# Where a router's logits are computed: from the transposed sum, or in parts beside q, k and the attention output

## The chip, the cores and the metric

The kernel runs on one core of one Trainium2 chip. Its time is the device time of one execution in microseconds (us). The profile shows one execution of 1613.6 us. Engines are named as in the profile: PE (matrix products), PEld (its weight loads), DVE (vector), ACT (scalar, activations), POOL, and SP, which issues most transfers.

## The reference

One layer over 4096 tokens of 256 features: a dense graph step, then attention, then a mixture of 8 experts of which each token takes two.

```python
x = x + concat([ln(x), adj @ (ln(x) @ neigh_W.T) / deg], -1) @ lin_W.T   # deg = adj row sums + 1
x0 = layernorm(x)                       # no weights
h = rmsnorm(x0, ln1_w)
q, k, v = h @ wq.T, h @ wk.T, h @ wv.T  # 4 heads, 2 of k and v, 64 wide; q and k are rotated
y = causal_softmax(q @ k.T / 8) @ v     # per head
x2 = x0 + y @ wo.T
flat = rmsnorm(x2, ln2_w)               # x2 / sqrt(mean(x2 * x2) + 1e-6) * ln2_w
probs = softmax(flat @ router_w.T)      # 4096 x 8
# the two best of each token, scaled to a sum of 1, weigh the experts
out = sum_e weight_e * ((silu(flat @ w1[e].T) * (flat @ w3[e].T)) @ w2[e].T)
return x + x2 + out
```

What the change uses is that the router is linear in x2 up to one factor per token, the one of the second rmsnorm. So its logits are that factor times (x0 @ R + y @ (wo.T @ R)), where R is router_w.T with its rows scaled by ln2_w.

## The kernel before

All data are float32. The tokens are eight blocks of 512 (`NB`), each four tiles (`TB`) of 128 rows (`P`). The order of the instructions on every engine is the order in which the program issues them; nothing reorders them afterwards. Loops take dictionaries or lists of small functions (`steps`, `later`, `rest`) and call them at set points between the big products, so an operation's place in the stream is written out by hand.

**Graph stage** (`aggregate`, L428). For each block of rows, eight blocks `jb` of the adjacency are multiplied with features, with seven products in place of eight per pair of blocks (`PRODUCTS`). After the seventh pair of products of every `jb` the functions of `steps[jb]` are called. In the first row block these make the features of the next block (`features`, L390; `turned_x`), and `load_rest` at `jb` 3 issues the loads of the attention's weights on SP. In row blocks 1 to 7 they are `qkv` of the block before: statistics at `jb` 0, the normalised input `h0` at 1 (DVE), its transposes at 2 (`transposed`, L321, with two scaled copies by ACT for each half, L329), then per tile `rotate` (one product with 512 columns for q, k and v, L184; v copied out by ACT, L188; the rotation on DVE and POOL) and `turn_heads` (`heads`: three transposes, L212, two copies by ACT, L213 and L214). At the end of a row block ACT copies the first product (L448), and DVE adds up the others and divides by the degrees; a bank of PSUM becomes free for the next row block when its part has been read.

**Attention** (L564 scores, L569 exponentials on ACT, L587 sums on DVE, L599 values). It goes through the blocks in the order 3, 0, 4, 1, 5, 2, 6, 7; the scores of one group of four tiles are issued before the values of the group before. There are two places for other steps in each group, `place_for_steps(2n)` and `(2n+1)`. `last_qkv` brings in block 7's q, k and v in the first of them. `after(b)` lists what follows a finished block: its input normalised again (`inputs`), the output product added (`project`, L634, L638), then `turn` (L653, L657, L666), `logits` (L681), `weigh` (L696), `choose`, `place` and `scatter`, the last four of which pick each token's experts and write its row into lists in memory. Steps that begin with `None` may share a place; the others each take one. All steps that use TensorE outside of scores and values share one bank of PSUM (`p_ms`).

Before, `turn` transposes x2, four 128x128 transposes for half a block, copies them out scaled by ln2 (ACT, into `qT[b]`, which the finished block's q no longer needs), and squares x2 on ACT for the rmsnorm; `logits` then multiplies `qT[b]` with `router_sb`:

```python
                    nc.tensor.matmul(
                        ps[32 * t : 32 * (t + 1), :], router_sb[:, c, :],
                        qT[b][:, c, t * P : (t + 1) * P],
```

The eight results of a token stand in partitions, so `weigh` transposes them back (L694) and multiplies with the factor of the rmsnorm, which POOL makes of the squares (`power`).

**Experts** (L1185 hidden, L1156 and L1237 output, L1094 transposes of a group's rows). Groups of 256 or 128 rows run one after another. While the first nine of them run, the steps of block 7's `after` are called one at a time by `step()`, two inside `hidden`, one behind it and one behind `combine`, and then two calls of `make_table` (DVE) that list the remaining groups. SP issues the loads of rows, `w13` and `w2` in program order. In the first six groups the transposes of the next group's rows share the bank `p_y` with the output product of the group before.

Of the kernel before, what the change touches and what calls it, by code (L numbers as in the profile page):

```python
# [17 lines left out]
P = 128  # L18
N = 4096
C = 256  # L20
# [46 lines left out]
def fast_kernel(  # L67
# [55 lines left out]
    wo_sb = const.tile([P, 2, C], F32, name="wo_sb")  # L123
    wqkv_sb = const.tile([P, 2, 512], F32, name="wqkv_sb")

    router_sb = const.tile([P, 2, 32], F32, name="router_sb")
    nc.gpsimd.memset(router_sb, 0.0)
# [19 lines left out]
    rstd = [const.tile([P, TB, 1], F32, name=f"rstd{b}") for b in range(NB)]  # L147
    both = [const.tile([P, TB, 1], F32, name=f"both{b}") for b in range(NB)]

    x_blocks = x.rearrange("(b t p) c -> b p t c", t=TB, p=P)  # L150
# [29 lines left out]

    def rotated(pool, b, t, hT, pj, ro, r2, cs, sn):

        for c in range(2):
            nc.tensor.matmul(  # L184
                pj, hT[:, c, t * P : (t + 1) * P], wqkv_sb[:, c, :],
                start=(c == 0), stop=(c == 1),
            )
        nc.scalar.copy(vv[b][:, t, :], pj[:, 384:512])  # L188
        qk = pj[:, 0:384].rearrange("p (h s d) -> p h s d", s=2, d=HD // 2)
        nc.vector.tensor_mul(  # L190
            ro.rearrange("p h s d -> p (h s) d"), qk.rearrange("p h s d -> p (h s) d"),
            cs.to_broadcast([P, 12, HD // 2]),
        )
        for s in range(2):
            nc.vector.tensor_mul(  # L195
                r2[:, :, s, :], qk[:, :, 1 - s, :], sn.to_broadcast([P, 6, HD // 2])
            )
        nc.gpsimd.tensor_sub(ro[:, :, 0, :], ro[:, :, 0, :], r2[:, :, 0, :])  # L198
        nc.gpsimd.tensor_add(ro[:, :, 1, :], ro[:, :, 1, :], r2[:, :, 1, :])
        sq = r2.rearrange("p h s d -> p h (s d)")  # L200
        rh = ro.rearrange("p h s d -> p h (s d)")
        nc.gpsimd.tensor_mul(sq, rh, rh)
        nm = pool.tile([P, 6, 1], F32, tag="nm", name=f"nm_{b}_{t}")
        nc.vector.tensor_reduce(nm, sq, AX.X, ALU.add)
        nc.vector.tensor_max(norms, norms, nm.rearrange("p h o -> p (h o)"))

    def heads(b, t, ro, tr):

        rof = ro.rearrange("p h s d -> p (h s d)")
        trf = tr.rearrange("p a b i -> p (a b) i")  # L210
        for m in range(3):
            nc.tensor.transpose(trf[:, m, :], rof[:, m * P : (m + 1) * P], ident)  # L212
        nc.scalar.copy(qT[b][:, :, t * P : (t + 1) * P], trf[:, 0:2, :])  # L213
        nc.scalar.copy(kT[b][:, t * P : (t + 1) * P], trf[:, 2, :])  # L214


    with (
# [50 lines left out]
        def load_rest():  # L268

            nc.sync.dma_start(wqkv_sb, wqkv.rearrange("(c p) o -> p c o", p=P))  # L270
            nc.sync.dma_start(ln1_sb, ln1)
            nc.sync.dma_start(ln2_sb, ln2)

            wo_h = wo_t.rearrange("(j p d) o -> j d p o", j=2, p=2)
            for j in range(2):
                nc.sync.dma_start(wo_sb[j * HD : (j + 1) * HD], wo_h[j])
            nc.sync.dma_start(
                router_sb[:, :, 0:NE], router_t.rearrange("(c p) e -> p c e", p=P)
            )
# [34 lines left out]

        def transposed(src, dst, scale):

            for h in range(2):
                tr = p_tr.tile([P, 2, 2, P], F32, tag="tr", name="tr")
                for t in range(2):
                    for c in range(2):  # L320
                        nc.tensor.transpose(  # L321
                            tr[:, c, t, :], src[:, 2 * h + t, c * P : (c + 1) * P], ident
                        )
                cols = slice(h * 2 * P, (h + 1) * 2 * P)
                if scale is None:
                    nc.scalar.copy(dst[:, :, cols], tr.rearrange("p c t i -> p c (t i)"))
                else:
                    for c in range(2):
                        nc.scalar.activation(  # L329
                            dst[:, c, cols], tr[:, c].rearrange("p t i -> p (t i)"),  # L330
                            AF.Copy, scale=scale[:, c : c + 1],
                        )

# [14 lines left out]
        def turned_x(b):  # L348
            turned[b] = qT[b % 4]
            transposed(inputs.pop(b), turned[b], None)  # L350

# [114 lines left out]
        def qkv(b):  # L466
# [9 lines left out]
            def norm():  # L476
                made["h0"] = gx.tile([P, TB, C], F32, tag="f", name=f"h0_{b}", bufs=1)
                for t in range(TB):
                    normed(made["h0"][:, t, :], b, t, both[b][:, t])

            def turn():

                made["hT"] = qT[b]
                transposed(made["h0"], made["hT"], ln1_sb)

            def rotate(t):
# [6 lines left out]
                    gx, b, t, made["hT"], pj, ro, r2,  # L493
                    tables[b, "cos"][:, t, None, :], tables[b, "sin"][:, t, None, :],
                )
                made[t] = ro

            def turn_heads(t):
                tr = p_tr.tile([P, 2, 2, P], F32, tag="tr", name=f"trq_{b}_{t}")
                heads(b, t, made.pop(t), tr)  # L500

# [26 lines left out]
        for jb in range(NB):  # L528
            for f, b in ((features, jb + 1), (turned_x, jb + 2), (halve, jb + 1), (scales_x, jb + 3)):
                if b < NB or f is halve:  # L530
                    steps[jb].append(lambda f=f, b=b: f(b))
        steps[3].append(load_rest)
        aggregate(0, steps)
        for b in range(1, NB):
# [5 lines left out]
    with (  # L540
# [105 lines left out]

        def turn(b, h):

            x2 = flats[b][:, :, 0:C]
            tr = p_ms.tile([P, 2, 2, P], F32, tag="ms", name=f"trf_{b}_{h}")  # L650
            for t in range(2):
                for c in range(2):
                    nc.tensor.transpose(  # L653
                        tr[:, c, t, :], x2[:, 2 * h + t, c * P : (c + 1) * P], ident
                    )
            for c in range(2):
                nc.scalar.activation(  # L657
                    qT[b][:, c, h * 2 * P : (h + 1) * 2 * P],
                    tr[:, c].rearrange("p t i -> p (t i)"),
                    AF.Copy, scale=ln2_sb[:, c : c + 1],  # L660
                )
            if h == 0:
                squares[b] = ax.tile([P, TB, 1], F32, tag="ss", name=f"ss_{b}")
            for t in range(2 * h, 2 * h + 2):
                sq = ax.tile([P, C], F32, tag="sq", name=f"sq_{b}_{t}", bufs=1)
                nc.scalar.activation(sq, x2[:, t, :], AF.Square, accum_out=squares[b][:, t])  # L666
            if h == 1:
# [8 lines left out]
        def logits(b):  # L676

            ps = p_ms.tile([P, P], F32, tag="ms", name=f"lgT_{b}")
            for c in range(2):
                for t in range(TB):  # L680
                    nc.tensor.matmul(  # L681
                        ps[32 * t : 32 * (t + 1), :], router_sb[:, c, :],
                        qT[b][:, c, t * P : (t + 1) * P],
                        start=(c == 0), stop=(c == 1), skip_group_check=True,
# [3 lines left out]
            nc.scalar.copy(lgT, ps)  # L688
            picks[b] = squares.pop(b), lgT

        def weigh(b):
            ri, lgT = picks[b]
            lg = p_ms.tile([P, TB, 32], F32, tag="ms", name=f"lg_{b}")
            nc.tensor.transpose(lg.rearrange("p t e -> p (t e)"), lgT, ident)  # L694
            pr = small("r_p", b)
            nc.vector.tensor_mul(pr, lg[:, :, 0:NE], over(ri))  # L696
            top = small("r_top", b, 1)
# [42 lines left out]
        def place(b):  # L740
# [19 lines left out]
            for i, oh in ((0, oh1), (1, oh2)):  # L760
                at = small("r_at", b)
                nc.vector.tensor_mul(at, oh, place)
# [46 lines left out]
        def after(b):  # L809
# [5 lines left out]
                [lambda: project(b, 1)],  # L815
                [lambda: turn(b, 0)],
                [lambda: turn(b, 1), lambda: residual(b)],
                [lambda: logits(b)],
                [lambda: weigh(b)],
# [12 lines left out]
        def last_qkv():  # L832
# [8 lines left out]
            def norm():  # L841
                made["h0"] = ax.tile([P, TB, ROW], F32, tag="row", name="h0_l")
                for t in range(TB):
                    normed(made["h0"][:, t, 0:C], b, t, both[b][:, t])

                made["hT"] = qT[b]

            def turned(h):
                tr = p_ms.tile([P, 2, 2, P], F32, tag="ms", name=f"tr_l{h}")
                for t in range(2):  # L850
                    for c in range(2):
                        nc.tensor.transpose(
                            tr[:, c, t, :], made["h0"][:, 2 * h + t, c * P : (c + 1) * P], ident
                        )
                for c in range(2):
                    nc.scalar.activation(
                        made["hT"][:, c, h * 2 * P : (h + 1) * 2 * P],
                        tr[:, c].rearrange("p t i -> p (t i)"),
                        AF.Copy, scale=ln1_sb[:, c : c + 1],
                    )  # L860

            def rotate(t):
# [7 lines left out]
                )  # L870
                rotated(ax, b, t, made["hT"], pj, ro, r2, cos_l[:, t, None, :], sin_l[:, t, None, :])
                made[t] = ro

            def turn_heads(t):
                tr = p_ms.tile([P, 2, 2, P], F32, tag="ms", name=f"trq_l{t}")
                heads(b, t, made.pop(t), tr)

# [1224 lines left out]
```

## Time and profile before

| | before |
|---|---|
| timed runs, median of three | 1615.77 us (1614.09 to 1616.06) |
| profiled span | 1613.6 us |
| PE busy | 1596.8 us, 99% |
| DVE busy | 1012.8 us, 63% |
| ACT busy | 490.2 us, 30% |
| POOL busy | 413.0 us, 26% |
| L653 transposes of x2 | 64, from 640.2 to 1122.7 us |
| L657 scaled copies of them | 32, 13.6 us of ACT |
| L666 squares | 32, 13.6 us of ACT, and 6.4 for their sums |

The busy time of PE is the time in which at least one product is in flight, so it says where PE idles, and not how much one product costs. A product of float32 is recorded as two passes, a transpose as one. A wait is put down to what ended it.

### The profile page before, as it was taken

The page shows a single profiled execution, that of the slowest core. Times are in us where ns is not written, and L with a number is a line of the kernel's source. Part 1 is how long each engine was busy: PE and PEld are TensorE (multiplying, and loading weights), DVE is VectorE, ACT ScalarE, POOL GpSimd, SP SyncE. Part 2 cuts the span into 40 slices and gives each one's busy share as a digit, 9 for nine tenths or more (in the row PEclk, how much of TensorE's full clock was granted, in tenths as well). Part 3 has the DMA queues.
Part 4 walks back from the last instruction along what each step waited for, and adds up shares of the span by engine and source line. Part 5 has one row for each costly group of instructions (what it writes and reads, how often), then busy time and mean ns, then how long its engine had stood idle before and what let it go on. Part 6 is the DMA issues. An engine that isn't in the chain of part 4 may idle for free.

```text
span 1613.6 us, 25682 instructions
## 1 busy us (share of the span) xinstructions
PE 1596.8 (99%) x9920; PEld 1162.6 (72%) x9920; DVE 1012.8 (63%) x2135; ACT 490.2 (30%) x933; POOL 413.0 (26%) x606
## 2 busy tenths in 40 slices
PE   9999999999999999999999999999999999999997
PEld 6779999999999544434434433437889999999996
DVE  5656656756665679778976977794355534435352
ACT  2110100000100455545465555543212222222221
POOL 1001111112112230453442441222522122221213
PEclk9999999999999999999999999999999999999999
DMA  6224434444444000001000010047766777777775
GB/s 228 99 79 144 150 131 160 144 139 144 160 134 135 4 0 1 23 31 37 32 31 23 28 41 1 14 166 232 221 199 182 227 252 254 242 248 229 254 259 120
DMA packets 67732, 209.79 MB, mean 130 GB/s; under 512 B 14672, under 2 KB 46288, under 8 KB 53968
## 3 DMA queue, kind: packets, MB, share of 16 engines
q1 hardware_dynamic: 54336, 190.05, 34.5%
q0 software_dynamic: 12720, 17.47, 5.5%
q8 instruction: 80, 1.31, 0.3%
q10 hardware_dynamic: 544, 0.52, 0.1%
q14 instruction: 52, 0.43, 0.1%
HBM read 180.81 MB, written 31.42 MB: 132 GB/s over the span
## 4 chain that ended last, share of the span: by engine, by line
PE 95%; DVE 2%; ACT 1%; DMA 0%; POOL 0%; issue 0%; SPq 0%; DVEq 0%; POOLq 0%; ACTq 0%
PE acc L428 25%; PE h L1185 20%; PE ya L599 14%; PE sc L564 13%; PE ye_y L1237 5%; PE pf L390 3%; PE pq L184 3%; PE ye_y L1156 3%; PE ye_ms L1156 2%; PE po L634 2%; DVE sum L587 1%; ACT pt L569 1%; PE tx L1094 1%; PE dn L612 1%; PE tr L321 1%; PE trq L212 1%
## 5 line engine op out<-in xcount | busy, mean ns | idle before, releaser
L587 DVE TENSOR_TENSOR sum<-sum,pt 128x1024 f32<-128x1024 f32 (+3 forms) x258 | 292.1, 1132 | 19.1 <-DVE sum L587 0.9
L569 ACT ACTIVATE pt<-sc 128x1024 f32<-128x1024 f32 (+3 forms) x288 | 251.5, 957 | 155.7 <-PE sc L564 118.6
L564 PE MATMUL sc<-qT_all,kT 64*128 64x512 f32 (+3 forms) x1152 | 251.9, 570 | 4.5 <-ACT pt L569 3.7
L428 PE MATMUL acc<-g,a 128*128 128x128 f32 x2048 | 255.7, 275 | 0.0
L599 PE MATMUL ya<-pt,vv 128*64 128x512 f32 (+3 forms) x1152 | 244.3, 566 | 0.0
L428 PEld LDWEIGHTS acc<-g,a 128*128 128x128 f32 x2048 | 241.8, 192 | 0.0
L1185 PE MATMUL h<-xT,qT_all 128*128 128x256 f32 (+1 forms) x1232 | 225.8, 342 | 0.0
L1185 PEld LDWEIGHTS h<-xT,qT_all 128*128 128x128 f32 x1232 | 200.0, 191 | 21.2 <-issue 1.0
L564 PEld LDWEIGHTS sc<-qT_all,kT 64*128 64x128 f32 x1152 | 103.3, 186 | 141.1 <-issue 104.0
L1192 DVE TENSOR_TENSOR hT<-si,h 128x256 f32<-128x256 f32 (+2 forms) x126 | 62.8, 507 | 191.3 <-ACT si L1191 190.1
L599 PEld LDWEIGHTS ya<-pt,vv 128*64 128x64 f32 x1152 | 76.7, 137 | 145.8 <-issue 140.3
L1257 POOL DMA_INDIRECT acc_dram<-y,rows x59 | 92.9, 1574 | 316.7 <-DVE y L1252 187.8
L1191 ACT ACTIVATE si<-h 128x256 f32<-128x256 f32 (+2 forms) x126 | 57.1, 454 | 272.9 <-PE h L1185 256.1
L1185 PE MATMUL h<-xT,res_all 128*128 128x256 f32 (+1 forms) x616 | 103.6, 327 | 0.0
L428 PE MATMUL acc<-g,more_sums 128*128 128x129 f32 (+1 forms) x768 | 101.7, 275 | 0.6 <-DVE more_sums L381 0.6
L792 POOL DMA_INDIRECT lists<-row,slots x64 | 72.7, 1136 | 114.7 <-issue 112.2
L428 PEld LDWEIGHTS acc<-g,more_sums 128*128 128x128 f32 x768 | 94.6, 192 | 7.5 <-issue 7.5
L1185 PEld LDWEIGHTS h<-xT,res_all 128*128 128x128 f32 x616 | 93.2, 191 | 8.0 <-issue 0.2
L428 PE MATMUL acc<-g,qT_all 128*128 128x128 f32 (+1 forms) x512 | 74.0, 274 | 0.0
L198 POOL TENSOR_TENSOR ro<-ro,r 128x192 f32<-128x192 f32 x28 | 16.5, 590 | 218.6 <-DVE r L195 218.6
L428 PEld LDWEIGHTS acc<-g,qT_all 128*128 128x128 f32 x512 | 66.5, 192 | 7.2 <-issue 7.2
L618 DVE RECIPROCAL rden<-rden 128x512 f32<-128x512 f32 x16 | 53.6, 3350 | 24.3 <-ACT rden L617 24.2
(263 smaller groups left out, 1929.7 us busy)
## 6 DMA issues: line engine op xcount, KB each, us to landing
a<-in_adj_dram SPq DMA_DIRECT2D x64, 1024.0 KB
qT_all<-in_w_dram SPq DMA_DIRECT2D x28, 1408.0 KB
res_all<-in_w_dram SPq DMA_DIRECT2D x28, 768.0 KB
res_all<-in_w_dram SPq DMA_DIRECT2D x14, 1408.0 KB
qT_all<-in_w_dram SPq DMA_DIRECT2D x14, 768.0 KB
rows<-lists SPq DMA_DIRECT2D x25, 265.0 KB
lists<-pad SPq DMA_DIRECT2D x8, 662.5 KB
acc_dram<-res_all SPq DMA_DIRECT2D x8, 512.0 KB
```

Source lines behind the costliest of these rows:

```text
L428: nc.tensor.matmul(acc[t][bank][:, at : at + w], m[left][:, k, t * P : (t + 1) * P], g[jb][:, right, k, 0:w], start=(jb == 0 and k == 0 an ...
L564: nc.tensor.matmul(ps[:, j, :w], kT[sb][hd, i * P : (i + 1) * P], qT[b][hd, p, off:], start=True, stop=True,)
L569: nc.scalar.activation(pt[:, :, :w], ps[:, :, :w], AF.Exp, scale=HD ** -0.5)
L587: nc.vector.tensor_add(sums[b, p][:, :, off:], before[:, :, off:], pt[:, :, : 512 - off])
L599: nc.tensor.matmul(accs[b, p][hd, off:], vv[sb][:, i, hd], pt[:, j, : 512 - off], start=(s == 0), stop=(s == TB * b + TB - 1),)
L792: put = nc.gpsimd.indirect_dma_start(out=lists[:, :], out_offset=bass.IndirectOffsetOnAxis(ap=chosen[b][:, k, t, :], axis=0), in_=flats[b] ...
L1156: nc.tensor.matmul(p[number], m[left][:, j, :], m[right][:, j, :], start=(n % 4 == 0 and j == 0), stop=(j == 2), skip_group_check=True,)
L1185: nc.tensor.matmul(ps[:, m % 2, m // 2 - q, :], w13_sb[:, c, m * P : (m + 1) * P], xT[:, c, :], start=(c == 0), stop=(c == 1),)
L1191: nc.scalar.activation(si[:, 0:both, :], ps[:, 0, 0:both, :], AF.Silu)
L1192: nc.vector.tensor_mul(hT[:, q : q + both, :], si[:, 0:both, :], ps[:, 1, 0:both, :])
L1237: nc.tensor.matmul(ps[h if last else 0][:, h, :], hT[:, q, cols], w2_sb[:, q, :], start=(q == 0), stop=(q == NF),)
L1257: put = nc.gpsimd.indirect_dma_start(out=(acc_dram if k < NM - LAST else out)[:, :], out_offset=at, in_=y[:, h, :], in_offset=None, comput ...
```

## The change

The router's weights, scaled by ln2, become eight columns of the same array as q's, k's and v's weights (`wqkv_sb`: 384 columns of q and k, 8 of the router, 128 of v). The scaling by ln1 and ln2, done on the transposed input before, is done once on the weights (`scale_rest`). The product in `rotated` gives q, k and the router's part of the attention's input; this input was scaled for the first rmsnorm, so ACT multiplies the part with the quotient of the two factors (`ratio`, DVE) when it copies it to `first_lg`. The product for v goes to `heads`, into the free quarter of the bank of its transposes, and is copied out there. In the first row block, `turn_wo` and `router_wo` compute wo times the router's weights into `router_sb`, once. `logits` multiplies that with the attention output `ys`, which is already transposed, and `weigh` adds `first_lg`. `turn` is gone; the squares of it stay as `squared`.

```diff
-                pj, hT[:, c, t * P : (t + 1) * P], wqkv_sb[:, c, :],
+                pj[:, 0 : QK + NE], hT[:, c, t * P : (t + 1) * P], wqkv_sb[:, c, 0 : QK + NE],
                 start=(c == 0), stop=(c == 1),
             )
-        nc.scalar.copy(vv[b][:, t, :], pj[:, 384:512])
+        nc.scalar.activation(
+            first_lg[b][:, t, :], pj[:, QK : QK + NE], AF.Copy, scale=unscale[:, t]
+        )
...
+        for c in range(2):
+            nc.tensor.matmul(
+                trf[:, 3, :], hT[:, c, t * P : (t + 1) * P], wqkv_sb[:, c, QK + NE :],
+                start=(c == 0), stop=(c == 1),
+            )
         for m in range(3):
             nc.tensor.transpose(trf[:, m, :], rof[:, m * P : (m + 1) * P], ident)
...
+        nc.scalar.copy(vv[b][:, t, :], trf[:, 3, :])
...
-            nc.sync.dma_start(wqkv_sb, wqkv.rearrange("(c p) o -> p c o", p=P))
+            w = wqkv.rearrange("(c p) o -> p c o", p=P)
+            nc.sync.dma_start(wqkv_sb[:, :, 0:QK], w[:, :, 0:QK])
+            nc.sync.dma_start(wqkv_sb[:, :, QK + NE :], w[:, :, QK:])
...
+        def turn_wo():
...
+                    nc.tensor.transpose(
+                        tr[:, c, j, :], wo_sb[:, j, c * P : (c + 1) * P], ident
+                    )
+            nc.scalar.copy(transposed_wo, tr.rearrange("p c j i -> p c (j i)"))
...
+        def router_wo():
...
+                    nc.tensor.matmul(
+                        ps[:, j * NE : (j + 1) * NE], transposed_wo[:, c, j * P : (j + 1) * P],
+                        wqkv_sb[:, c, QK : QK + NE], start=(c == 0), stop=(c == 1),
+                    )
...
+        for jb, f in ((5, scale_rest), (6, turn_wo), (7, router_wo)):
+            steps[jb].append(f)
...
-        def turn(b, h):
...
+        def squared(b, h):
...
             for t in range(2 * h, 2 * h + 2):
-                sq = ax.tile([P, C], F32, tag="sq", name=f"sq_{b}_{t}", bufs=1)
-                nc.scalar.activation(sq, x2[:, t, :], AF.Square, accum_out=squares[b][:, t])
+                nc.scalar.activation(
+                    qT[b][:, 0, 0:C], flats[b][:, t, 0:C], AF.Square, accum_out=squares[b][:, t]
+                )
...
-                        qT[b][:, c, t * P : (t + 1) * P],
+                        ys[b, c][:, t * P : (t + 1) * P],
...
-            nc.vector.tensor_mul(pr, lg[:, :, 0:NE], over(ri))
+            nc.vector.tensor_add(pr, lg[:, :, 0:NE], first_lg[b])
+            nc.vector.tensor_mul(pr, pr, over(ri))
...
-                [lambda: turn(b, 0)],
-                [lambda: turn(b, 1), lambda: residual(b)],
-                [lambda: logits(b)],
+                [lambda: logits(b), lambda: squared(b, 0)],
+                [None, lambda: squared(b, 1), lambda: residual(b)],
+                [None],
                 [lambda: weigh(b)],
```

Block 7's step of transposing its input (`last_qkv`) is changed in the same way: one plain copy in place of two scaled ones.

## The prediction

> **What bounds the kernel now.** I read the page first: the busy times, then the chain that ended last.
>
> ```profile
> PE 1596.8 (99%) x9920; PEld 1162.6 (72%) x9920; DVE 1012.8 (63%) x2135; ACT 490.2 (30%) x933; POOL 413.0 (26%) x606
> PE 95%; DVE 2%; ACT 1%; DMA 0%; POOL 0%; issue 0%; SPq 0%; DVEq 0%; POOLq 0%; ACTq 0%
> ```
>
> TensorE is busy almost without a gap, and 95% of the chain is its own work. So TensorE time taken out of the stream counts, unless another engine is close behind. To see where one is, the busy time by stage (graph, attention, experts; columns: length, then PE, PEld, DVE, ACT, POOL busy with counts):
>
> ```profile
> 117.00:537.00 420.00, 419.45 (x3436) 392.60 (x3436) 262.92 (x626) 36.49 (x128) 80.84 (x112) 1.00 0.43 141
> 537.00:1097.00 560.00, 555.44 (x2718) 222.66 (x2719) 450.42 (x691) 299.39 (x434) 189.99 (x279) 1.00 0.11 35
> 1097.00:1590.00 493.00, 493.00 (x3075) 452.81 (x3072) 226.11 (x619) 130.25 (x317) 119.43 (x151) 1.00 0.74 233
> ```
>
> Attention is the only stage with another engine near: DVE, 450 of 560 us (80%). PE idles 4.6 us there, and the waits (total, times, longest) give 3.7 of it to ACT:
>
> ```profile
> PE sc L564 <- ACT pt L569: 3.7, 4, 1.7
> ```
>
> What one instruction is worth on PE is not its duration (they overlap) but the distance between starts, which the chain shows as merged pieces. Attention, around the transposes that go (start, us, what):
>
> ```profile
> 640.29 0.59 PE trf L653 x4
> 640.88 3.58 PE ya L599 x16
> 644.46 0.60 PE trf L653 x4
> ...
> 646.86 0.92 ACT pt L569
> 647.78 0.04 issue
> 647.83 0.49 PE sc L564 x4
> 648.32 0.57 PE lgT L681 x16
> ```
>
> Four transposes take 0.59 us out of the stream. Between 644.46 and 647.83 the chain leaves PE: ACT does the scaled copies and squares of L657 and L666 ahead of the exponentials, and PE waits 0.64 us for a score bank. The graph stage, same columns:
>
> ```profile
> 153.89 1.72 PE pq L184 x4
> 155.61 6.25 PE acc L428 x56
> 161.86 0.33 PE trq L212 x3
> ```
>
> An fp32 product is recorded as two passes, a transpose as one. A 512-wide pass is 1.72/4 = 0.430 us, a 128-wide one 6.25/56 = 0.1116, a transpose 0.33/3 = 0.11.
>
> **What the Trainium skill says.** "TensorE: Matmul & The Clock Gate", Part 4: PE-mode transpose, gives about 275 ns for one; the trace has 273 as the duration but 0.11 as the spacing, so pricing 64 of them by duration (17.5 us) would be twice too much. "TensorEngine Tiling (Array Packing)", Key Properties, says that changing the tiling mode drains TensorE. The trace agrees: scores and values use 64-row or 64-column tiles, and four transposes between them cost 0.59; between full-array products in the expert stage they cost 0.44 (1119.38 to 1119.82):
>
> ```profile
> 1119.38 0.60 PE L653 MATMUL trf<-ident,row 128*128 128x128 f32 x4
> 1119.82 2.76 PE L1185 MATMUL h<-xT,qT_all 128*128 128x256 f32 x12
> ```
>
> **The change part by part.**
>
> Removed: trf. Eight blocks times two times four transposes. Fourteen groups are in attention: 14 x 0.59 = -8.3 us. Block 7's two are in the expert stage: 2 x 0.44 = -0.9. With them go 32 scaled copies (L657, 13.6 us of ACT). The squares (L666) stay, but no longer wait behind a transpose; in the changed instruction order the logits stand where the first transposes stood, so both pairs of squares follow at once and are done before the next scores. Of the four ACT waits, the two of 0.64 us (647.83 and 701.80) directly follow L657/L666: -1.3. The other two remain.
>
> Logits: same 8 products at the same tile positions, moved two slots earlier, reading yT, which is finished by then: 0.
>
> Split product: q, k and router columns are 392 wide, v becomes two products of 128 in the heads step. Between the two measured widths a column costs (0.430-0.1116)/384 = 0.83 ns, so a 392-wide pass is 0.330 us. One tile: 4 x 0.330 + 4 x 0.1116 = 1.77 against 1.72; 32 tiles: +1.5 us. Bounds: +0.9 (no cost for the weight loads) to +12.8 (rival two).
>
> ACT in that step: v's copy (0.27) moves, and a scaled [128x8] copy is new. "ScalarE: Activation LUTs", What ACT_TABLE_LOAD costs, prices an immediate copy at 186 ns + 0.833 per element and a pointer scale at 93 more: an estimate of 0.29 us. The trace agrees on the pointer: 475 against 377 ns for 256 columns. Against it, the two ln1-scaled copies of 0.475 become one of 0.59. ACT is 9% busy in the graph stage, so this is hidden, except at block ends: there the copies of two heads stand before the copy L448 that starts the sums of the aggregate, and the next block's third product waits for the end of that chain (slack 0.49 us at 182.97, almost none at 186.10). Working that queue through, the chain starts 0.96 us later and PE gets there 0.89 later: 0.07 x 6, +0.4 with rounding (0 to 1).
>
> Once only. SP issues one more DMA (0.44 us) ahead of an adjacency load that goes out at 74.94, ten us later: hidden. Six scalings of weights on ACT, about 2.4 us by the rates above, in this gap:
>
> ```profile
> 107.79 0.37 ACT L397 COPY g<-pf 128x256 f32<-128x256 f32 x1 [7.28 <-PE pf L390]
> ```
>
> They wait for loads issued by about 65 us; behind them stands only that copy. turn_wo's four transposes (0.44) come before a PE wait of 0.64 us at 117.55 for DVE's sums: 0 (at most 0.44). router_wo: 8 passes of 8 columns. Nearest row: four 32-wide passes (pl) from 1147.92 to 1148.28, 0.09 each; so 0.7. "TensorE: Matmul & The Clock Gate", Back-to-back issue gap, has a floor of 25 ns, which gives 0.2; the trace's 0.09 decides, upper end 0.9.
>
> DVE: two tiny operations per block for the ratio (0.18 each, graph stage 63% busy: hidden) and one more add per block in weigh. The wait of 1.71 us at 717.35 is an exponential queued on ACT behind weigh's result (the chain runs through r_p), so there +0.2.
>
> Expert stage: block 7's steps come one earlier. No PE wait is there to win. But the second table now stands on DVE ahead of y of the fourth group (y_3), whose bank the next transposes need:
>
> ```profile
> 1175.46 0.88 DVE L1252 TENSOR_SCALAR y<-ye_y,gt 128x256 f32<-128x256 f32 x2
> 1176.26 0.17 DVE L959 TENSOR_TENSOR left<-run,base 128x8 f32<-128x8 f32 x1
> 1178.16 0.60 PE L1094 MATMUL tx<-ident,rows 128*128 128x128 f32 x4
> ```
>
> The two tables take 3.6 us (1171.46 to 1175.0) and 4.5 us (1176.26 to 1180.72). The first can now start after the hidden product that ends at 1168.45, so: 1168.45 + 3.6 + 0.9 (two small products) + 4.5 + 1.3 (y) = 1178.75, against 1178.16 when PE needs the bank: +0.6 (0 to 1). On POOL two scatters go ahead of that group's sums; SP then issues a row load and the weights behind it about 3 us later, still two groups before their use.
>
> Sum: -8.3 - 0.9 - 1.3 + 1.5 + 0.4 + 0.7 + 0.2 + 0.6 = **-7.1 us**. Against the profiled span of 1613.6 that is 1606.5; the median of the timed runs is 2.2 above that span and falls alike: 1615.8 - 7.1 = **1608.7**.
>
> **The rivals.** A measurement of this kernel can tell about 0.2% (3.2 us) from no change.
>
> One: DVE takes the gain in attention. It is 80% busy there, and in places (583 to 607, 707 to 716) the chain already runs along it. If each of the 14 groups taken out only let PE reach a sum earlier, the 8.3 us would become waits: net +1.2, about 1617. Against it: the stretches that run along DVE start from a PE product (dn) that comes after the transposes of 695 and 698, so they move along. For it: what is not on the chain is not shown. Chance 0.11.
>
> Two, slower: the narrowed product isn't cheaper. If the 392-wide pass took 0.430 like the 512-wide one, each tile would cost 0.40 more: 12.8 us, net +5.7, about 1621.5. It decides from 0.330 + 7.1/128 = 0.385 us per pass. Against it, the value products by width in attention (busy, mean ns):
>
> ```profile
> L599 PE MATMUL ya<-pt,vv 128*64 128x384 f32 x64 | 13.0, 486 | 0.0
> L599 PE MATMUL ya<-pt,vv 128*64 128x256 f32 x64 | 9.6, 379 | 0.0
> ```
>
> At 512 it is 604, so durations fall in proportion. Chance 0.06.
>
> Three: more than the sum. If ACT's relief also removed the remaining waits of PE (2.4 us) and the expert wait of 0.6 did not come, 1605.5. Chance 0.10.
>
> That the change doesn't do what it says is excluded: the changed order has no trf, 64 more 128-wide products and the 392-wide ones.
>
> **How the numbers follow.** The sum as worked out, within its bounds (1606.5 to 1611.5), has 0.73. The range, 1605.5 to 1613, adds rival three and part of rival one. Faster by over 0.2% is the sum, rival three and a little of rival one: 0.84. Within 0.2% is most of rival one: 0.10. Slower is rival two: 0.06.
>
> **What would show it.** Right: trf gone; attention shorter by about 9.5 us; graph stage longer by 1.5 to 3; pq pieces of 1.32 and v-plus-transposes pieces of 0.78; two ACT waits of 0.64 gone; a short wait before a tx near 1170. Wrong: pq pieces well above 1.32; PE idle in attention above 4.6 us with DVE sums as releasers; a new wait at the block ends of the graph stage.

## The result and the profile after

| | before | after |
|---|---|---|
| timed runs, median of six each | 1615.91 us (1613.91 to 1618.39) | 1607.80 us (1606.12 to 1613.24) |
| ratio | | 0.9957, interval 0.9939 to 0.9974 |
| profiled span | 1613.6 us | 1609.0 us |
| graph stage, to the first score product | 537.0 us | 539.1 us |
| attention, to the first hidden product | 560.3 us | 549.2 us |
| experts, to the start of the last output product | 507.2 us | 507.9 us |
| tail, from there to the end | 9.1 us | 12.8 us |

The forecast was 1608.7 us. The ratio is that of the means of the six, which are 7.0 us apart; the medians are 8.1 apart. The profiled execution of after took 1610.77 us, the second slowest of its six. The stages are cut at the starts of PE's products, so they add up to the span. First the busy times and the first line of the chain of the page of after:

```profile
PE 1588.1 (99%) x9996; PEld 1171.8 (73%) x9996; DVE 1020.6 (63%) x2159; ACT 484.0 (30%) x925; POOL 417.0 (26%) x606
PE 93%; DVE 3%; ACT 1%; issue 1%; DMA 1%; POOL 0%; SPq 0%; DVEq 0%; POOLq 0%; ACTq 0%
```

PE has 76 more instructions and 8.7 us less busy time. The 2% by which PE's share of the chain fell tell nothing by themselves: a second profile of the kernel before has 93% too. The busy times by stage (length, PE, PEld, DVE, ACT, POOL), as before:

```profile
117.00:539.00 422.00, 421.80 (x3559) 406.05 (x3557) 264.85 (x639) 38.50 (x143) 80.86 (x112) 1.00 0.41 140
539.00:1088.00 549.00, 544.42 (x2681) 218.87 (x2681) 456.24 (x700) 289.89 (x409) 193.93 (x279) 1.00 0.11 36
1088.00:1585.00 497.00, 495.83 (x3083) 454.76 (x3080) 226.75 (x621) 129.56 (x314) 119.37 (x150) 1.00 0.73 230
```

In attention PE is busy for 11 us less and still idles 4.6 us: DVE, now 83% busy, did not take the gain. (Of the 11 us, 1.7 are not the change's: PE's clock was low for a moment in the profile of before, see the last section.) The waits of PE in after (total, times, longest), part of the list:

```profile
PE sc L617 <- ACT pt L622: 2.3, 2, 1.9
...
PE po L687 <- DVE row L691: 1.4, 1, 1.4
...
PE tx L1140 <- DVE y L1298: 0.6, 1, 0.6
```

Waits for ACT fell from 3.7 to 2.3. The wait before `po` looks new, and the one before `tx` is; a wait of 0.5 us before an output product (`ye_y`, at 1507.65) is in this profile of after and not in the second one. The chain in the graph stage (start, us, what):

```profile
154.33 1.32 PE pq L197 x4
155.65 6.25 PE acc L477 x56
161.90 0.45 PE trq L227 x4
162.34 0.33 PE trq L232 x3
```

The product of q, k and the router takes 1.32 where the 512-wide one took 1.72; v's 0.45 is beside the three transposes. In attention, at the place where the first transposes of x2 stood:

```profile
642.75 0.57 PE lgT L724 x16
643.32 3.58 PE ya L652 x16
646.91 1.08 PE sc L617 x4
```

The logits took the place of four transposes of 0.59, and at 646.91 the scores follow the values directly, where before another 0.59 and then a wait of 0.64 followed.

At the end of the kernel, the POOL timeline of after has the sums on `out` in pairs, one pair for a group. These start the first and the last of the four pairs (start, duration, what, in brackets the idle time before and what ended it):

```profile
1581.54 1.57 POOL L1303 DMA_INDIRECT out_dram<-y,rows  x1 [25.18 <-ACT si L1237]
...
1600.93 1.57 POOL L1303 DMA_INDIRECT out_dram<-y,rows  x1 [2.84 <-DVEq L2069]
```

The pairs start 6.4 to 6.6 us apart, because each waits until the one before has landed, and the first waits for the copy of `acc_dram` into `out`, issued at 1564.44. The bracket names DVE, but the last output products ended by 1596.6, and the chain shows what came last: the landing of the sums issued at 1596.41, 3.79 us later. In the kernel before, the last pairs did wait for their own y:

```profile
1597.89 1.57 POOL L1257 DMA_INDIRECT out_dram<-y,rows  x1 [4.35 <-DVE y L1252]
...
1605.52 1.57 POOL L1257 DMA_INDIRECT out_dram<-y,rows  x1 [3.35 <-DVE y L1252]
```

So PE was done 8.3 us earlier in this execution (the last output product started at 1596.2 instead of 1604.5), and 3.7 us of it went into a longer tail.

### The profile page after: what moved, and what is told of

It is laid out like the page before. It is cut to its first block, busy times and chain, and to the rows that moved or that the text cites. A ratio compares the mean times of both kernels' runs of the same rounds, so it can differ in the third digit from the quotient of the medians.

```text
span 1609.0 us, 25844 instructions
## 1 busy us (share of the span) xinstructions
PE 1588.1 (99%) x9996; PEld 1171.8 (73%) x9996; DVE 1020.6 (63%) x2159; ACT 484.0 (30%) x925; POOL 417.0 (26%) x606
## 4 chain that ended last, share of the span: by engine, by line
PE 93%; DVE 3%; ACT 1%; issue 1%; DMA 1%; POOL 0%; SPq 0%; DVEq 0%; POOLq 0%; ACTq 0%
PE acc L477 25%; PE h L1231 20%; PE ya L652 14%; PE sc L617 13%; PE ye_y L1283 5%; PE pf L439 3%; PE ye_y L1202 3%; PE pq L197 2%; PE ye_ms L1202 2%; PE po L687 2%; ACT pt L622 1%; DVE sum L640 1%; PE tx L1140 1%; PE trq L227 1%; PE tr L377 1%; PE dn L665 1%
## 5 line engine op out<-in xcount | busy, mean ns | idle before, releaser
L640 DVE TENSOR_TENSOR sum<-sum,pt 128x1024 f32<-128x1024 f32 (+3 forms) x258 | 298.1, 1155 | 19.5 <-DVE sum L640 1.4
```

What stands on the lines that cost most here:

```text
L640: nc.vector.tensor_add(sums[b, p][:, :, off:], before[:, :, off:], pt[:, :, : 512 - off])
```

## The experiments

Expectations speak of theory one and theory two. Every ratio is to the kernel before, timed beside the run. A difference in time to after's 1607.80 us goes across two sets of timed runs and is less sure.

**The kernel before, profiled again**, for the wait before `po`.

> The kernel before, unchanged, for a second profile. In the first one the clock of PE was down to 0.9 from 712 to 728 us, which cost 1.7 us there, and PE met the sums of DVE at 747.7 us without a wait. Theory one (the wait of 1.4 us at 746.9 us in the changed kernel is older than the change, and the slow stretch hid it before): without a slow stretch at that place the output product po of that block waits some 1.2 to 1.6 us for DVE here too, and PE idles 4.9 to 5.3 us in attention. Theory two (the wait came with the change, by the transposes taken out): no wait at that product, and PE idles 3.7 us in attention as before.

One run, 1615.34 us. The wait of 1.4 us for `row` is in it, so it is older than the change. In the first profile of before, PE's granted clock was 0.89 on the mean from 712 to 728, the value product at 717.77 took 5.35 us for 16 passes instead of 3.65, and the 1.7 us lost there hid the later wait. Either way the stage takes the same: 560.3 and 560.6 us.

**The split product alone**: the products, copies and scaling of after; `turn`, `logits`, `weigh` and the order of before. The new logits are computed and not used.

```diff
-        for jb, f in ((5, scale_rest), (6, turn_wo), (7, router_wo)):
+        for jb, f in ((5, scale_rest),):
...
-                [lambda: logits(b), lambda: squared(b, 0)],
-                [None, lambda: squared(b, 1), lambda: residual(b)],
-                [None],
+                [lambda: turn(b, 0)],
+                [lambda: turn(b, 1), lambda: residual(b)],
+                [lambda: logits(b)],
```

> The projections arranged as in the changed kernel (392 columns for q, k and the router's part, v as two products of 128 in the step of the heads, weights scaled once), but the logits made as before, from the transposed sum; the router's part is computed and not used. Theory one (the split costs little, the gain is all in the transposes): the graph stage is longer than before by 0.5 to 1.5 us, attention as before, so +1 to +2 us in all, 0.1%. Theory two (part of the gain comes from the new arrangement, by the lighter ACT): attention gets shorter by 1 us or more, and the whole is at or below the time before.

1616.88 us beside 1615.41, ratio 1.0002 (0.9994 to 1.0011). The graph stage is 1.3 to 1.4 us longer and attention unchanged at 560.3. The split costs little, and the gain isn't in it.

**v kept in the wide product**, the router's eight columns as the product of their own:

```diff
-                pj[:, 0 : QK + NE], hT[:, c, t * P : (t + 1) * P], wqkv_sb[:, c, 0 : QK + NE],
+                pj, hT[:, c, t * P : (t + 1) * P], wqkv_sb[:, c, NE : NE + 512],
...
-                trf[:, 3, :], hT[:, c, t * P : (t + 1) * P], wqkv_sb[:, c, QK + NE :],
+                trf[:, 3, 0:NE], hT[:, c, t * P : (t + 1) * P], wqkv_sb[:, c, 0:NE],
```

> The changed kernel with the eight columns of the router as a product of their own, in the step of the heads, and q, k and v in one product of 512 columns as before. Theory one (columns cost 0.83 ns each pass, and a thin pass has a floor near 0.09 us): a tile costs 1.72 + 4 x 0.09 to 0.11 in place of 1.77 us, so 0.31 to 0.39 us more, and with 32 tiles 10 to 12.5 us more than the changed kernel: about 1619, slower than before. Theory two (the floor of a thin pass is some 25 ns): 1.82 us a tile, 1.6 us more than the changed kernel.

1618.68 us, ratio 1.0013 (1.0005 to 1.0021), and 10.9 us more than after: theory one. The graph stage is 548.9, 9.8 us longer than after's. PE's timeline there:

```profile
162.50 0.51 PE L225 MATMUL trq<-wqkv_sb,qT_all 128*128 128x8 f32 x4
162.87 0.52 PE L230 MATMUL trq<-ident,ro 128*128 128x128 f32 x3
163.23 1.88 PE L197 MATMUL pq<-wqkv_sb,qT_all 128*128 128x512 f32 x4
```

From start to start, four passes of 8 columns take 0.37 us, 0.09 each, and four of v's 128 columns 0.45. A sixteenth of the columns saves a fifth. The floor of 25 ns, which the prediction took from the Trainium skill ("TensorE: Matmul & The Clock Gate", Back-to-back issue gap), is far from these 90 ns a pass, so the measurement decides. Moving v, which the wide product pays for at its full rate, is what makes the router's columns cheap: the place of the split is worth more than the whole change.

**The transposes back**, two steps of four as before, into a bank that nothing reads; the logits two places later, without the scaled copies:

```diff
-                [lambda: logits(b), lambda: squared(b, 0)],
-                [None, lambda: squared(b, 1), lambda: residual(b)],
-                [None],
+                [lambda: extra(b, 0), lambda: squared(b, 0)],
+                [lambda: extra(b, 1), lambda: squared(b, 1), lambda: residual(b)],
+                [lambda: logits(b)],
```

> The changed kernel with the sixteen groups of four transposes put back where they stood, with nothing that reads them (no copies out), and the logits two places later as before. Theory one (PE sets the time in attention, and each group costs it 0.59 us there and 0.44 in the experts): 14 x 0.59 + 2 x 0.44 = 9.1 us more than the changed kernel by the busy stretches, 8 to 10 in the time. Theory two (DVE is the bound behind PE, and part of the time taken out comes back as waits): under 6 us more, with fewer waits of PE for DVE and ACT in attention than in the changed kernel.

1615.53 us, ratio 1.0001 (0.9994 to 1.0009): 7.7 us more than after, and the time of the kernel before. Theory one asked for 8 to 10, theory two for under 6; the spacing of the transposes, below, is theory one's. Attention is 558.3, 9.1 longer than in after and 7.8 longer than in its second profile. Its chain:

```profile
646.97 0.59 PE trf L707 x4
647.56 1.08 PE sc L618 x4
```

The transposes cost 8.2 us of spacing in the stage (14 x 0.59; the first four stand at 642.80), and at 647.56 the scores come without a wait although the transposes stand there again: the wait of 0.64 went with the scaled copies on ACT and the place of the squares behind them, not with the transposes on PE. So both parts of the gain are separate. Beyond the 8.2, a wait of 0.77 at 852.49 is in this profile and in the second of after, but not in the first; the wait at 701.80 is gone here, and is 0.41 in after. In this profile of after the tail is 12.8, here 9.8, so the spans are only 5.4 apart.

**The changed kernel again, and the copy one group earlier** in both kernels. In the fourth, an empty step keeps the last table off the y that `tx` waits for.

```diff
-LAST = 4
+LAST = 5
...
+            [lambda: None],
             [lambda: make_table(NB, True, NA, NW - NA)], [lambda: make_table(NB, False, NW, NG - NW)],
```

> The changed kernel once more, timed beside the three kernels that follow, so that their tails have a second profile of it to stand against. Theory one (the end is bound by the copy of acc_dram into out and by the four groups' sums on out that follow it one after the other): the first sum on out starts 16 to 18 us after the copy is issued, the four groups' sums 6 to 7 us apart, the tail after the last product 11 to 13 us; 1607 to 1609 us. Theory two (the long tail was one execution's chance): the tail is 9 to 10 us again, with the last sums waiting for ACT and DVE.

> The changed kernel with LAST = 5 instead of 4: the copy of acc_dram into out is issued one group earlier, and five groups' sums go to out. Theory one (the end waits for the copy and the chain of sums behind it): the chain has some 13 us more, the last sums wait for their own y, the tail is 9 to 10 us instead of 12.8, and the time falls by 2.5 to 4 us, to 1604 to 1605.5. Theory two (the tail is as long for another reason, such as the load on the DMA engines): the tail stays near 12.8 and the time within 1 us of the changed kernel's.

> As copy_earlier, and with one empty step ahead of the two that make the last two tables, so that these stand one group later on DVE and not ahead of the y that the tx copy waits for. Theory one (PE's wait of 0.62 us before the first tx is that y behind a table): the wait goes, 0.4 to 0.8 us less than copy_earlier. Theory two (the wait is in the turn of transposes and copies, whatever stands before): the wait stays at 0.5 to 0.7 and the time is copy_earlier's within 0.5.

> The kernel before with LAST = 5. Theory one (before, PE's work ended late enough that its last sums waited for their own y and not for the copy): no gain, within 1 us of the kernel before, tail 9 to 10 us. Theory two (the copy costs both kernels the same): 2.5 to 4 us less than before, as for the changed kernel.

| | us | ratio | last output product | first sum on `out` | tail |
|---|---|---|---|---|---|
| after_again | 1609.87 | 0.9964 (0.9952 to 0.9975) | 1596.7 | 1574.3 | 9.6 |
| copy_earlier | 1613.72 | 0.9983 (0.9976 to 0.9990) | 1602.4 | 1568.7 | 9.8 |
| copy_and_tables | 1611.02 | 0.9969 (0.9956 to 0.9982) | 1600.3 | 1566.2 | 9.0 |
| before_copy_earlier | 1619.06 | 1.0015 (1.0006 to 1.0023) | 1605.4 | 1570.8 | 8.9 |

No theory stood as a whole. In after_again the copy was issued at 1558.12, the first sum started 16.2 us later, and the end waited for the last y: tail 9.6. So the 12.8 is not in every execution. The copy one group earlier kept the tail at 9 to 10 us, but both kernels became slower by 3 to 4 us, which neither theory expected. `LAST` also goes into `TURNS`, the order of the groups, so the edit changed two things. The profile of copy_earlier shows where PE stood, before the copy was issued at 1553.05:

```profile
1497.60 2.63 PE L1202 MATMUL ye_y<-qT_all,hT 128*128 128x128 f32 x12 [3.57 <-DVE y L1298]
```

and on DVE's timeline, six instructions ahead of that y in its queue:

```profile
1494.42 0.56 DVE L1178 TENSOR_TENSOR vv<-qT_all 128x384 f32<-128x384 f32 x1 [4.57 <-DMA qT_all<-in_w_dram]
```

DVE waited 4.57 us for a group's weights, y stood behind that, and PE behind y. Right after it PE's clock was low for 3.4 us (last section), which cost another 1.7: together 5.3 of the 5.7 us by which PE ended later than in after_again. That a wait of this kind is typical of the other order isn't shown by one profile each. The profile of before_copy_earlier, of an execution 3 us under its median, has no such wait. What made the two kernels slower stays open. copy_and_tables has no wait before the first `tx`, as theory one said, but three others (1.44 at 1494.34, 1.64 at 1574.56 and 0.61 at 1578.51).

**The copy cut to one row, in both kernels; the copy one group later; the empty step alone.**

```diff
-                nc.sync.dma_start(out, acc_dram[0:N, :])
+                nc.sync.dma_start(out[0:1, :], acc_dram[0:1, :])
```

> The changed kernel with its copy of acc_dram into out cut to one row: all but that row of the sums of the other groups is missing from the output, and 4 MB less is moved beside the last weights. Theory one (a part of the gain is lost at the end, where the sums on out stand behind the copy and PE's last products are done): the first sum on out starts about 12 us earlier, each later sum waits only for its own y, the tail is 9 us and the time 1605 to 1606.5, 2 to 4 us under the changed kernel. Theory two (the end is set by the last y alone, the profile with the 12.8 was chance): within 1 us of the changed kernel beside it.

> The kernel before with the same cut: all but one row of the other groups' sums is missing from the output. Theory one (before, PE ended 8 us later, so its last sums waited for their y and not for the copy): within 1 us of the kernel before, and the distance between the two kernels without the copy is the 8 us that PE's work became shorter. Theory two: the copy costs both kernels the same, 2 to 4 us, and the distance stays at 6.5 to 7.

> The changed kernel with LAST = 3 instead of 4: the copy is issued one group later, behind the last load of w2, and three groups' sums go to out. Theory one (copy_earlier was slower because the 4 MB of the copy met the loads of w2 that follow it, and at LAST = 4 a part of that is left): PE's experts stage is 506.5 to 507.5 with no new wait, the chain on out has one pair less, and the time is within 1.5 us of the changed kernel on either side. Theory two (the copy and what follows it bound the end, and the loads don't matter): the copy is 10 to 12 us later, one pair of 6.5 us is saved, and the time rises by 3 to 6 us.

> The changed kernel with one empty step ahead of the two that make the last two tables, LAST as it is. Theory one (the wait of 0.62 us before the first tx stands behind a table on DVE): the wait goes or shrinks to 0.2, 0.3 to 0.7 us less than the changed kernel. Theory two (a table on DVE makes PE wait wherever it stands, as the 1.6 us wait for DVE in copy_and_tables suggests): another wait of 0.5 to 1.6 us comes in its place, and the time is the changed kernel's or up to 1.5 us more.

| | us | ratio | last output product | first sum on `out` | tail |
|---|---|---|---|---|---|
| no_copy | 1607.50 | 0.9947 (0.9929 to 0.9966) | 1597.2 | 1566.9 | 9.3 |
| before_no_copy | 1614.86 | 0.9998 (0.9984 to 1.0011) | 1604.2 | 1575.6 | 9.0 |
| copy_later | 1609.07 | 0.9958 (0.9944 to 0.9973) | 1595.8 | 1586.4 | 12.4 |
| tables_later | 1608.06 | 0.9951 (0.9935 to 0.9966) | 1595.4 | 1578.5 | 10.3 |

The end is the later of two: with four groups on `out`, the first sum plus 27 us (after 1581.5 to 1609.0, tables_later 1578.5 to 1605.7), or the last output product plus 9 (after_again, no_copy, all profiles of before). They meet when the first sum is some 18 us ahead of the last product: before, 21 and 23 us, just free; after, 14.7 in one profile and 22.4 in the other. (thin_product and transposes_back, both with 18.4, have tails of 10.3 and 9.8, so the rule is good to about 1 us.)

The change moved PE's end to where the first can win. That is theory one's mechanism, but its mean cost is not resolved: no_copy missed the 1605 to 1606.5, its interval overlaps the changed kernel's, and the two kernels without the copy are 7.4 us apart where they are 6.3 to 8.1 with it. before_no_copy lies 1.9 us under the median of the kernel before beside it, but its interval takes in no change, so it doesn't tell the theories apart. In copy_later the first sum on `out` came 5 to 12 us later, one pair was saved, PE had no new wait, and the time can't be told from the changed kernel's: theory one, not the 3 to 6 us of theory two, though this edit too reorders the groups. That the copy met loads of weights in copy_earlier is not shown by it, since the wait found there came before the copy.

The empty step alone did what it was meant to. PE in tables_later:

```profile
1165.82 3.40 PE L1231 MATMUL h<-xT,res_all 128*128 128x256 f32 x15
1169.06 0.60 PE L1140 MATMUL tx<-ident,rows 128*128 128x128 f32 x4
```

As theory one expected, no wait stands before `tx`, and none came in its place: PE idles 0.0 us in the expert stage, against 1.2 and 0.6 in the two profiles of after. 1608.06 us beats the kernel before; that it beats the changed one is not resolved.

## Why the prediction was right, point by point

The terms can be measured one by one: for each kind of product, the distances from each start to the next start on PE, summed over a stage. "Before" has two profiles, "after" two. For attention there are more: before_copy_earlier and before_no_copy have its code of before, and thin_product, copy_earlier, copy_and_tables, no_copy, copy_later and tables_later have that of after.

| step | forecast | measured |
|---|---|---|
| transposes gone, attention | -8.3 | -8.2 (8.21 to 0) |
| transposes gone, experts | -0.9 | -0.9 (0.87 to 0) |
| ACT waits, and +0.2 for `weigh` | -1.1 | -2.0, place by place (below); the scores' distances in all go from 250.5 to 252.2 down to 248.6 to 249.6 |
| split product | +1.5 | +1.3 in the graph stage (57.30 to 58.59), +0.4 for block 7 (9.57 to 9.93) |
| block ends | +0.4 | 0 |
| `turn_wo` | 0 | 0: 0.44 of its own, and the wait at 117.55 fell from 0.64 to 0.20 |
| `router_wo` | +0.7 | +0.8 |
| wait before `tx` | +0.6 | 0.6 of idle time, +0.9 in the distances of `h` (321.3 to 322.2) |
| PE's end | -7.1 | -8.3 and -8.0 (1604.5 and 1604.7 to 1596.2 and 1596.7) |
| time | -7.1 | medians -8.1, and -6.3 with the second set; by the ratios -7 and -6 |

The steps held, and the two that carry the sum, 0.59 a group of transposes and 0.330 a pass of 392 columns, to the second digit: pq is 1.32, as 4 x 0.330. That the whole came within 1 us is in part luck: 0.9 us more gained at ACT's waits and 0.4 less lost at the block ends stand against 0.2 more lost for the split, 0.1 for `router_wo` and 0.3 for `tx`, and some waits come and go between executions. (The 275 ns that the prediction quotes for a transpose are the page's figure for bf16 data; the float32 ones here have 273. ACT's new copy of 8 columns, estimated at 0.29 us, took 0.27.) The two places where it went wrong:

The term of the ACT waits was mis-sized. "the two of 0.64 us (647.83 and 701.80) directly follow L657/L666: -1.3. The other two remain" is not what came. The wait at 647.83 went. That at 701.80 only fell to 0.41, and `weigh` added the forecast 0.2 to the longest:

```profile
701.65 0.49 PE L617 MATMUL sc<-qT_all,kT 64*128 64x128 f32 x4 [0.41 <-ACT pt L622]
716.85 0.49 PE L617 MATMUL sc<-qT_all,kT 64*128 64x128 f32 x4 [1.93 <-ACT pt L622]
```

At 701 the second pair of squares is still ahead of the exponentials on ACT, from 699.63 to 700.59; the text had them "done before the next scores".

What the prediction missed are five more places, which no list of waits shows. At 760, 808, 870, 926 and 1025 us of before, too, the scaled copies and squares held up the exponentials, and a score bank came late. But PE's earlier products were still in flight when it came, so PE counts as idle for 3 ns at most by the profile. The distances between starts show it: twice 0.42 us became 0.59 and 0.53. One of the five, before:

```profile
758.04 3.98 PE L564 MATMUL sc<-qT_all,kT 64*128 64x512 f32 x16
759.83 2.83 ACT L569 ACTIVATE pt<-sc 128x1024 f32<-128x1024 f32 x3
```

and the same place after:

```profile
756.61 3.70 PE L617 MATMUL sc<-qT_all,kT 64*128 64x512 f32 x16
757.79 2.85 ACT L622 ACTIVATE pt<-sc 128x1024 f32<-128x1024 f32 x3 [1.84 <-PE sc L617]
```

From the start of the scores to that of the exponentials it is 1.79 us before and 1.18 after, and the same scores take 0.28 us less. In before, the late scores at 760.89 start 0.05 us after the first of these exponentials has ended. In all five places the 0.27 us are in split_only, which has the scaled copies, and gone in transposes_back, which hasn't. So the term is -0.6 at 647.83, -0.2 at 701.80, +0.2 for `weigh` and five times -0.27, -2.0 in all. The wait of 0.73 at 851.59, which after's first profile lacks, is not the change's: before_no_copy lacks it too, and after_again has 0.80 there.

The tail was not in the working at all. The prediction took an earlier end of PE for an earlier end of the kernel. Behind PE's last product stood a chain of transfers that was only 3 to 5 us from setting the end, and it moves with the transfers, not with PE. In the profile of after, that took back 3.7 of the 8.3 us; in the second one it took back about 0.5. How much it is on the mean is not resolved.

Rival one has no support: PE's idle time in attention did not grow, and no new wait for DVE came there, although DVE's sums (`sum`) take 298.1 us instead of 292.1, in transposes_back too and not in split_only; why is open. Rival two is excluded by the pieces of 1.32. The durations that it was weighed with (604, 486 and 379 ns) do not fall in proportion to the columns, as the text said, but by 0.8 to 0.9 ns a column. Rival three's mechanism was partly real: more was gained on the ACT side than forecast, though not at the waits that it named, and the experts' wait came.

## What to carry to other kernels

Price a PE instruction by the distance between starts in the chain. When columns are split over two products, let the smaller product be a wide one: four passes of 8 columns cost four fifths of four passes of 128 here. A wait can cost time and leave no idle time behind, while products are in flight; comparing the distances of the same products in two profiles finds it. When PE sets the time, ask what ends the kernel once PE is done: a chain of dependent transfers a few microseconds short of the end can take the next gain. A constant that also orders other work is no clean experiment on the one thing that it is named for.

## What the runs showed that was not expected

In 9 of the 14 profiles (before and after_again among them) PE's granted clock was 0.50 for 3.4 us near 720; in the other 5 (before_again and after among them) it stayed at 1.00. In copy_earlier it sank at 1498 instead. The stretch in before, and the one in copy_earlier (columns as above, then the clock and the DMA engines' share and rate):

```profile
718.50:721.90 3.40, 3.40 (x10) 0.98 (x8) 3.12 (x12) 0.26 (x1) 3.35 (x7) 0.50 0.00 0
1498.10:1501.40 3.30, 3.30 (x17) 3.30 (x17) 1.02 (x5) 1.25 (x4) 1.69 (x2) 0.50 0.37 85
```

All ten stretches begin 0.2 to 1.6 us after PE has gone on from a wait of 1.7 us or more: the one for ACT at 717, and the one of 3.57 us in copy_earlier. No wait of up to 1.64 us was followed by one. But the same wait at 717 is in the 5 others as well, so what decides is not shown. The lower clock cost 1.7 us, and PE's wait of 1.4 us before `po` at 747 is in exactly the 5 profiles in which the clock did not sink near 720, so that attention took nearly the same either way.

The copy of 4 MB from one place in memory to another took 16.3 us to land beside the last loads of weights, and pairs of accumulating sums behind it started 6.4 to 6.6 us apart.
